# Layer 3 of a fused four-layer kernel: one key tile per work item, or two

## The chip, the cores and the metric

The kernel runs on one core of one Trainium2 chip, in one launch. Times are device microseconds of that core, from the median of three runs; the profile is of one further execution. The engines are named as the profile names them: PE (TensorE matmul) and PEld (its weight loads), ACT (ScalarE), DVE (VectorE), POOL (GpSimd) and SP (SyncE).

## The reference

Four layers follow each other on an input x of 4 images, 64 by 64 points and 64 channels, all in float32:

- layer 0: self-attention over the 4096 points of an image, with projections q, k, v; `x = gamma * out + x`
- layer 1: layer norm, pointwise and 3x3 depthwise convolutions, gates, a second layer norm and pointwise block, both with residuals
- layer 2: attention with x as query, key and value at once, in the (channel, row, column) reading of the same array; `out + x`
- layer 3: attention with 32 inner channels, then a projection back and a batch norm over all images, with a residual:

```python
f = softmax(theta_x @ phi_x.T)            # per image, 4096 x 4096
y = f @ g_x                               # 4096 x 32
w_y = y @ w_W + w_b
x + gamma * (w_y - mean) * rsqrt(var + EPS) + beta
```

The change concerns layer 3 alone.

## The kernel before, in words

The order of the work on PE, ACT and DVE is written out by hand. Each layer appends items to the list `items`; item i is called at step i, and the function `at(i, fn)` puts work into `due[i]`, which is called after item i in the same step, in the order in which it was put there. The instructions that these calls issue go into each engine's queue in that order. Two side lanes, `conv` and `misc`, hold generators (layer 1's convolutions; projections and closings of the attention layers) that are stepped between items: each item has a cost, the lanes' clocks advance by it twice per step, and a lane's next piece is issued when its clock has reached that piece's due time. `misc_from[i]` starts generators at step i; `misc_to[i]` drains the lane before it. Only the layers' order is fixed: layer 0 of all images, then layer 2 of image 0, and from there layer 2 of image b followed by layer 3 of image b − 1, and at the end layer 3 of image 3.

Layer 3 of an image runs over two halves `nb`. In each half the 2048 queries lie in four groups of 512, one for each of four row blocks of 32 partitions, and 32 key tiles `mc` of 128 keys follow each other: 64 tiles n per image. For a tile:

- `scores(n)` takes two PSUM buffers `ps` of 128x1024 from a pool of three, fills them with four matmuls of 32 rows by 128 columns (line 1314; the profile counts two instructions for each matmul), and turns each into exponentials with one ACT instruction (line 1319), both into one tile `e` of 128x2048, from a pool of six.
- `products(n)` multiplies e with g_x by four matmuls of 128 rows by 32 columns into the accumulator `y` (line 1327). The denominators of the softmax are the sums of e over all keys. For most tiles DVE adds e to a running tile, `esum` (lines 1340 and 1342); for the tiles mc = 9, 19 and 29, PE adds it instead, by four matmuls with ones into a second accumulator (line 1335).
- `totals`, once per half, adds the running tile to that accumulator with ones (line 1350), copies it out on ACT (1354), and forms the quotients on DVE (1355, 1356).
- `close` projects the result (1366), adds the bias on ACT (1368), and takes statistics on DVE (1370, 1372).

Tile n's scores are item n of the layer, cost 1.0; its products are due two items later, so PE's order is scores(n), products(n − 2), scores(n + 1), products(n − 1). Totals are due four items after the last tile of a half (two, at the end of images 0 and 1), and close eight items after it. The last tiles' products, totals and close of an image fall into the first items of what comes next. While layer 3 of image 2 runs, the lane `misc` works through `close2` and `open3` of image 3 (layer 2's normalization, and the projections that the next layer 3 needs); they are added 56 items before that layer 3 begins. `open3`'s pieces each take one more ps buffer, which DVE reads out.

Of the kernel before, what the change touches and what calls it, by code (L numbers as in the profile page):

```python
# [691 lines left out]
def fast_path(ctx: ExitStack, tc: tile.TileContext, a: dict, out: bass.AP, bad):  # L692
    nc = tc.nc
    B, H, W, C = a["x"].shape
# [16 lines left out]
    def new_ps(name="ps"):  # L711
        return pp.tile([128, 1024], F32, tag="ps", name=name)

    def new_acc(name="acc"):
        return pa.tile([128, 512], F32, tag="acc", name=name)

    def new_e(name="e"):
        return ep.tile([128, 2048], F32, tag="e", name=name)

    def new_t(name="t"):  # L720
        return tp.tile([128, 1024], F32, tag="t", name=name)

    def new_big(name):
        return big.tile([128, 4096], F32, tag="big", name=name)

    def new_pad(name="pad"):
        return big.tile([128, 66 * PW + 2], F32, tag="pad", name=name, bufs=1)
# [80 lines left out]
    for nm in names64 + names32:  # L808
        n = flat[nm].shape[0]
# [8 lines left out]
    def V(nm, i=0, lo=0, hi=128):  # L818
        k = col[nm] + i
        return vec[lo:hi, k : k + 1]  # L820
# [104 lines left out]
    def tok(x, s, j):  # L925
        return x[64 * s : 64 * s + 64, bass.ts(j, 512)]
# [4 lines left out]
    items, due = [], {}  # L931

    def at(i, fn):
        due.setdefault(i, []).append(fn)
# [316 lines left out]
    def close2(b):  # L1251
        x, m = X[:, b], im[b]
        nc.vector.tensor_reduce(sums2[:, b, :], m.zs, AX.X, ALU.add)
        rz = sm.tile([128, 32], F32, tag="rz2", name="rz2")
        nc.vector.reciprocal(rz, sums2[:, b, :])
        for i in range(4):
            d = m.ph[:, bass.ts(i, 512)].rearrange("p (w h) -> p w h", h=H)
            nc.vector.tensor_mul(d, d, rz[:, bass.ts(i, 8)].unsqueeze(2).to_broadcast([128, 8, H]))
            xs = x[:, bass.ts(i, 512)]
            nc.vector.tensor_add(xs, xs, m.ph[:, bass.ts(i, 512)])  # L1260
            yield 2.0
# [5 lines left out]
    def open3(b):  # L1267
        x, m = X[:, b], im[b]
        m.tg = new_big("tg")
        m.th = m.tg[:, 0:1024]  # L1270
        m.gx = m.tg[:, 1024:2048].rearrange("p (t d) -> p t d", d=32)
        ps = new_ps()
        for nb in range(2):
            for jj in range(2):
                mm(
                    ps[:, bass.ts(nb, 512)], thw[jj], x[:, bass.ts(2 * nb + jj, 512)],
                    start=jj == 0, stop=jj == 1,
                )
        nc.vector.tensor_scalar_add(m.th, ps, V("L3_conv_theta_b"))
        yield 3.5  # L1280
        for j in range(4):
            ps = new_ps()
            for s in range(2):
                mm(
                    ps[:, bass.ts(s, 512)], phw[64 * s : 64 * s + 64, :], tok(x, s, j),
                    start=True, stop=True,
                )
            nc.vector.tensor_scalar_add(
                m.ph[:, 0:N].rearrange("p (s n) -> p s n", s=2)[:, :, bass.ts(j, 512)],
                ps.rearrange("p (s n) -> p s n", s=2), V("L3_conv_phi_b"),  # L1290
            )
            yield 3.5
        ps = new_ps()
        for t in range(16):
            mm(ps[:, bass.ts(t, 64)], x[:, bass.ts(t, 128)], gw, start=True, stop=True)
        for s in range(2):
            nc.vector.tensor_add(
                m.gx[:, bass.ts(s, 16), :],
                ps.rearrange("p (t s d) -> p t s d", s=2, d=32)[:, :, s, :],
                gb.unsqueeze(1).to_broadcast([128, 16, 32]),  # L1300
            )
        yield 3.5

    def layer3(b):
        m, first = im[b], len(items)
        es, st = {}, {}

        def scores(n):
            nb, mc = n // 32, n % 32
            e = es[n] = new_e()  # L1310
            tiles = [new_ps(), new_ps()]
            for k in range(4):
                rows_ = slice(32 * k, 32 * k + 32)
                mm(  # L1314
                    tiles[k // 2][:, bass.ts(k % 2, 512)], m.ph[rows_, bass.ts(mc, 128)],
                    m.th[rows_, bass.ts(nb, 512)], start=True, stop=True,
                )
            for kp in range(2):
                act(e[:, bass.ts(kp, 1024)], tiles[kp], AF.Exp)  # L1319

        def products(n):
            nb, mc = n // 32, n % 32
            e, esum = es[n], m.tg[:, 2048:4096]
            if mc == 0:
                st["y"] = new_acc()
            for k in range(4):
                mm(  # L1327
                    st["y"][32 * k : 32 * k + 32, :], m.gx[:, mc, :], e[:, bass.ts(k, 512)],
                    start=mc == 0, stop=mc == 31,
                )  # L1330
            if mc % 10 == 9:
                if mc == 9:
                    st["z"] = new_acc("accz")
                for k in range(4):
                    mm(  # L1335
                        st["z"][32 * k : 32 * k + 32, :], ones[:, 0:32], e[:, bass.ts(k, 512)],
                        start=mc == 9, stop=False,
                    )
            elif mc == 1:
                nc.vector.tensor_add(esum, es[n - 1], e)  # L1340
            elif mc:
                nc.vector.tensor_add(esum, esum, e)  # L1342
            if mc == 31:
                st["yz"] = new_t("yz")
                nc.scalar.copy(st["yz"][:, 0:512], st["y"])  # L1345

        def totals():
            z, yz = st["z"], st["yz"]
            for k in range(4):
                mm(  # L1350
                    z[32 * k : 32 * k + 32, :], ones[:, 0:32], m.tg[:, 2048 + 512 * k : 2560 + 512 * k],
                    start=False, stop=True,
                )
            nc.scalar.copy(yz[:, 512:1024], z)
            nc.vector.reciprocal(yz[:, 512:1024], yz[:, 512:1024])  # L1355
            nc.vector.tensor_mul(yz[:, 0:512], yz[:, 0:512], yz[:, 512:1024])

        def close(nb):
            yz = st["yz"]
            if b % 2 == 0 and nb == 0:  # L1360
                wys["pair"] = new_big("wy") if b else new_pad("wy")
            if nb == 0:
                wys[b] = wys["pair"][:, bass.ts(b % 2, 2048)]
            ps = new_ps()
            for jj in range(2):
                mm(ps[:, bass.ts(jj, 512)], wo[jj], yz[:, 0:512], start=True, stop=True)  # L1366
            wy = wys[b][:, bass.ts(nb, 1024)]
            act(wy, ps, AF.Identity, bias=V("L3_conv_w_b"))
            for i in range(2):
                nc.vector.bn_stats(bst[:, b, nb, i, :], wy[:, bass.ts(i, 512)])  # L1370
            for i, op in enumerate((ALU.max, ALU.min)):
                nc.vector.tensor_reduce(ext3[:, b, nb, i : i + 1], yz[:, 512:1024], AX.X, op)

        for n in range(64):
            items.append((lambda n=n: scores(n), 1.0))
            at(first + n + 2, lambda n=n: products(n))
            if n % 32 == 31:
                at(first + n + (2 if n == 63 and b < 2 else 4), totals)
                at(first + n + 8, lambda n=n: close(n // 32))


    conv_from, misc_from, misc_to = {}, {}, {}
# [9 lines left out]
    for b in range(B):  # L1392
        misc_to[len(items)] = True
        f = len(items)
        layer2(b)
        more = [features2(b + 1)] if b + 1 < B else []
        if b == 0:
            misc_from[f + 16] = more
        else:
            misc_from[f + 3] = [close2(b - 1), open3(b - 1)]  # L1400
            misc_from[f + 22] = more
            misc_to[len(items)] = True
            layer3(b - 1)
    f = len(items)
    misc_from[f - 56] = [close2(B - 1), open3(B - 1)]
    misc_to[f] = True
    layer3(B - 1)

    def run():
# [83 lines left out]
    for i, (v, lo, hi) in enumerate(vals):  # L1493
        n = v.shape[1]
# [11 lines left out]
@with_exitstack  # L1506
def conv_seq_kernel(ctx: ExitStack, tc: tile.TileContext, a: dict, out: bass.AP):
    nc = tc.nc
    flag = ctx.enter_context(tc.tile_pool(name="flag", bufs=1))
    bad = flag.tile([1, 1], mybir.dt.int32, name="bad")  # L1510
    fast_path(tc, a, out, bad)
    n_bad = nc.values_load(bad[0:1, 0:1], min_val=0, max_val=1 << 20)
    with tc.If(n_bad > 0):
        general_path(tc, a, out)
# [37 lines left out]
```

## Time and profile before

| | |
|---|---|
| median of three runs | 2829.94 us (2826.72 to 2830.79) |
| the profiled execution | 2832.79 us |
| its span, first to last instruction | 2830.9 us |
| mean granted TensorE clock | 0.99 |
| busy: PE, ACT, DVE | 2746.0, 1742.7, 1443.4 us |
| layer 3 of image 0, from its first scores to the next layer's | 1675.32 to 1826.82 us |
| of image 1 | 2069.54 to 2222.47 us |
| of image 2 | 2459.45 to 2629.46 us |
| of image 3, to its last sums | 2629.46 to 2777.55 us |

A group line of the page names the source line, the engine and operation, what it writes and reads, its shape and count; then the busy time of the group and the mean of one in nanoseconds; then the engine's idle time ahead of it and what ended most of that. A timeline line has the start and the length of a merged row of instructions in microseconds, and in brackets the engine's idle time ahead of it with its releaser. Matmuls overlap, so a merged row reaches a little into the next. A line of waits has who waited, for whom, the total in microseconds, how often, and the longest.

### The profile page before, as it was taken

To read this page: it belongs to the slowest core of one execution; us is meant where nothing else is said; L and a number is where in the kernel's file an instruction comes from. 1 tells how busy PE (TensorE), PEld (TensorE's weight loads), DVE (VectorE), ACT (ScalarE), POOL (GpSimd) and SP (SyncE) were. 2 spreads that over 40 slices of the span, in tenths; PEclk is the share of its full clock that TensorE was granted. 3 is DMA by queue.
4 is the path that set the end of the run, shared out by engine and by line. 5 is a ranking of instruction groups with operands and counts; after the bars stand their busy time and mean duration, and the time that the engine had idled before them with its cause. 6 is when DMAs were issued, how large, how long until landed. Compare 5 with 4: busy or idle time off the path is not lost.

```text
span 2830.9 us, 41626 instructions
## 1 busy us (share of the span) xinstructions
PE 2746.0 (97%) x17950; PEld 929.1 (33%) x17950; DVE 1443.4 (51%) x1551; ACT 1742.7 (62%) x2807; POOL 21.5 (1%) x77
## 2 busy tenths in 40 slices
PE   8999999999999999989999999999999999999995
PEld 3343333333333333322333332243322333322222
DVE  3232488435794348521772128920068610198896
ACT  4545555555655565556645568845678656678884
POOL 2000000000000000000000000000000000000000
PEclk9999999999999999999999999999999999999997
DMA  4000000000000000000000000000000000000002
GB/s 70 1 1 1 1 1 1 1 0 1 1 1 1 1 0 1 1 1 1 1 1 1 1 1 1 1 1 1 1 1 1 1 1 1 1 1 1 1 1 61
DMA packets 18500, 11.80 MB, mean 4 GB/s; under 512 B 1436, under 2 KB 18181, under 8 KB 18309
## 3 DMA queue, kind: packets, MB, share of 16 engines
q1 hardware_dynamic: 16085, 7.89, 1.3%
q8 instruction: 142, 2.33, 0.3%
q10 hardware_dynamic: 1296, 0.56, 0.1%
q0 software_dynamic: 928, 0.62, 0.1%
q14 instruction: 49, 0.40, 0.0%
HBM read 4.87 MB, written 4.19 MB: 3 GB/s over the span
## 4 chain that ended last, share of the span: by engine, by line
PE 90%; DVE 6%; ACT 3%; issue 1%; DMA 0%; ACTq 0%; DVEq 0%; POOL 0%; POOLq 0%
PE acc L1034 16%; PE ps L1010 16%; PE acc L1224 16%; PE ps L1207 15%; PE ps L1314 9%; PE acc L1327 7%; DVE tg L1342 2%; PE ps L1161 2%; PE ps L1104 1%; PE ps L1061 1%; DVE yz L1355 1%; ACT e L1319 1%; PE ps L1366 1%; PE accz L1335 1%; PE ps L987 1%
## 5 line engine op out<-in xcount | busy, mean ns | idle before, releaser
L1014 ACT ACTIVATE e<-ps 128x1024 f32<-128x1024 f32 x512 | 516.9, 1024 | 343.2 <-PE ps L1010 208.9
L1215 ACT ACTIVATE e<-ps 128x1024 f32<-128x1024 f32 x512 | 517.0, 1024 | 317.3 <-PE ps L1207 316.9
L1319 ACT ACTIVATE e<-ps 128x1024 f32<-128x1024 f32 x512 | 495.9, 1023 | 110.4 <-PE ps L1314 92.0
L1342 DVE TENSOR_TENSOR tg<-tg,e 128x2048 f32<-128x2048 f32 x216 | 494.9, 2291 | 26.2 <-ACT e L1319 8.2
L1010 PE MATMUL ps<-X,q 64*128 64x512 f32 x2048 | 491.2, 606 | 13.4 <-ACT e L1014 4.2
L1207 PE MATMUL ps<-ko 64*64 64x512 f32 x4096 | 474.6, 596 | 18.1 <-ACT ko L1190 8.7
L1224 PE MATMUL acc<-e,X 64*64 64x512 f32 x4096 | 469.0, 593 | 0.6 <-ACT yz L1345 0.6
L1034 PE MATMUL acc<-e,vq 128*64 128x512 f32 x2048 | 468.4, 599 | 0.0
L1314 PE MATMUL ps<-tg,ph 32*128 32x512 f32 x2048 | 320.7, 640 | 5.6 <-ACT e L1319 4.2
L1041 DVE SCALAR_TENSOR_TENSOR yv<-acc,gam,yv 128x512 f32<-128x512 f32 x224 | 167.4, 749 | 242.8 <-PE acc L1034 231.3
L1010 PEld LDWEIGHTS ps<-X,q 64*128 64x128 f32 x2048 | 190.4, 186 | 293.6 <-issue 185.5
L1327 PE MATMUL acc<-e,tg 128*32 128x512 f32 x2048 | 272.4, 604 | 1.3 <-ACT yz L1345 1.3
L1207 PEld LDWEIGHTS ps<-ko 64*64 64x64 f32 x4096 | 152.5, 133 | 314.1 <-issue 196.8
L1224 PEld LDWEIGHTS acc<-e,X 64*64 64x64 f32 x4096 | 157.3, 133 | 282.6 <-issue 272.5
L1034 PEld LDWEIGHTS acc<-e,vq 128*64 128x64 f32 x2048 | 136.5, 137 | 312.0 <-issue 290.2
L1232 DVE TENSOR_TENSOR ph<-ph,acc 128x512 f32<-128x512 f32 x16 | 11.0, 687 | 389.1 <-ACT ph L1231 389.1
L1314 PEld LDWEIGHTS ps<-tg,ph 32*128 32x128 f32 x2048 | 102.5, 183 | 223.5 <-issue 147.3
L1126 DVE SCALAR_TENSOR_TENSOR y<-pad,vec,y 128x1024 f32<-128x1024 f32 x128 | 164.3, 1283 | 7.6 <-ACT pad L1109 3.5
L1126 DVE SCALAR_TENSOR_TENSOR yg<-pad,vec,yg 128x1024 f32<-128x1024 f32 x128 | 164.3, 1283 | 3.8
L1014 ACT ACTIVATION_READ_ACCUMULATOR e<-ps 128x1 f32 x512 | 106.0, 207 | 0.0
L1215 ACT ACTIVATION_READ_ACCUMULATOR e<-ps 128x1 f32 x512 | 106.0, 207 | 0.0
L1327 PEld LDWEIGHTS acc<-e,tg 128*32 128x32 f32 x2048 | 41.0, 108 | 196.3 <-issue 190.6
(177 smaller groups left out, 1221.9 us busy)
## 6 DMA issues: line engine op xcount, KB each, us to landing
out_dram<-o SPq DMA_DIRECT2D x16, 256.0 KB
xr<-in_x_dram SPq DMA_DIRECT2D x14, 256.0 KB
xr<-in_x_dram ACTq DMA_DIRECT2D x2, 256.0 KB
pw<-in_L_conv_pw_w_dram POOLq DMA_DIRECT2D x4, 64.0 KB, 4.9
phw<-in_L_conv_phi_W_dram POOLq DMA_DIRECT2D x8, 8.0 KB, 1.8
sca<-in_L_conv_sca_w_dram POOLq DMA_DIRECT2D x1, 64.0 KB, 6.3
pw<-in_L_conv_pw_w_dram POOLq DMA_DIRECT2D x2, 32.0 KB, 5.3
thw<-in_L_conv_theta_W_dram POOLq DMA_DIRECT2D x4, 8.0 KB, 2.1
```

What stands on the lines that cost most here:

```text
L1010: mm(ps[:, bass.ts(r, 512)], m.q[rows_, bass.ts(t, 128)], x[rows_, bass.ts(g, 512)], start=True, stop=True,)
L1014: act(es[g // 2][:, bass.ts(g % 2, 1024)], ps, AF.Exp, bias=SHIFT0, accum_out=zs[:, g : g + 1],)
L1034: mm(accs[g][64 * r : 64 * r + 64, :], vq, es[half][:, 1024 * g + 512 * r : 1024 * g + 512 * r + 512], start=t == 2 * p, stop=t == 2 * p + 1,)
L1041: stt((x if p == 15 else m.y)[:, cols], accs[g], gam0, (m.y if p else x)[:, cols], ALU.mult, ALU.add,)
L1126: stt(out_, win, wt, out_, ALU.mult, ALU.add)
L1207: mm(ps[64 * c : 64 * c + 64, bass.ts(r, 512)], m.ko[rows_, 128 * jb + 64 * c : 128 * jb + 64 * c + 64], m.ko[rows_, bass.ts(2 * ib + r, 5 ...
L1215: act(es[n, jb], ps, AF.Exp, bias=SHIFT2, accum_out=m.zs[:, jb, ib : ib + 1])
L1224: mm(acc[r][64 * c : 64 * c + 64, :], xw[rows_, jb, :], es[n, jb][rows_, bass.ts(c, 512)], start=jb == 0, stop=jb == 31,)
L1314: mm(tiles[k // 2][:, bass.ts(k % 2, 512)], m.ph[rows_, bass.ts(mc, 128)], m.th[rows_, bass.ts(nb, 512)], start=True, stop=True,)
L1319: act(e[:, bass.ts(kp, 1024)], tiles[kp], AF.Exp)
L1327: mm(st["y"][32 * k : 32 * k + 32, :], m.gx[:, mc, :], e[:, bass.ts(k, 512)], start=mc == 0, stop=mc == 31,)
L1342: nc.vector.tensor_add(esum, esum, e)
```

## The change

An item of layer 3 now holds two key tiles: their scores are issued one after the other, and in the same step the products of the two tiles in front. The tiles that PE sums are mc = 4, 9, 14, 19, 24 and 29, six per half in place of three, so DVE adds three tiles fewer. An item costs 2.0 on the lanes' clocks, so a tile costs what it did. Distances in items are halved: products come one item later, totals two (one, at the end of images 0 and 1), close four, and the lane work for image 3 is added 28 items ahead. Pools, tiles and shapes of all instructions stay.

```diff
-            if mc % 10 == 9:
-                if mc == 9:
+            if mc % 5 == 4:
+                if mc == 4:
                     st["z"] = new_acc("accz")
                 for k in range(4):
                     mm(
                         st["z"][32 * k : 32 * k + 32, :], ones[:, 0:32], e[:, bass.ts(k, 512)],
-                        start=mc == 9, stop=False,
+                        start=mc == 4, stop=False,
                     )
...
-        for n in range(64):
-            items.append((lambda n=n: scores(n), 1.0))
-            at(first + n + 2, lambda n=n: products(n))
-            if n % 32 == 31:
-                at(first + n + (2 if n == 63 and b < 2 else 4), totals)
-                at(first + n + 8, lambda n=n: close(n // 32))
+        for n in range(0, 64, 2):
+            i = first + n // 2
+            items.append((lambda n=n: [scores(n), scores(n + 1)], 2.0))
+            at(i + 1, lambda n=n: [products(n), products(n + 1)])
+            if n % 32 == 30:
+                at(i + (1 if n == 62 and b < 2 else 2), totals)
+                at(i + 4, lambda n=n: close(n // 32))
...
-    misc_from[f - 56] = [close2(B - 1), open3(B - 1)]
+    misc_from[f - 28] = [close2(B - 1), open3(B - 1)]
```

## The prediction, made before the changed kernel had run

> **What bounds the kernel now.** I read the page first, then the windows of layer 3's stages, then the PE and ACT timelines inside one stage, then single instruction starts. The page:
>
> ```profile
> PE 2746.0 (97%) x17950; PEld 929.1 (33%) x17950; DVE 1443.4 (51%) x1551; ACT 1742.7 (62%) x2807; POOL 21.5 (1%) x77
> PE 90%; DVE 6%; ACT 3%; issue 1%; DMA 0%; ACTq 0%; DVEq 0%; POOL 0%; POOLq 0%
> L1319 ACT ACTIVATE e<-ps 128x1024 f32<-128x1024 f32 x512 | 495.9, 1023 | 110.4 <-PE ps L1314 92.0
> L1342 DVE TENSOR_TENSOR tg<-tg,e 128x2048 f32<-128x2048 f32 x216 | 494.9, 2291 | 26.2 <-ACT e L1319 8.2
> ```
>
> PE carries 90% of the chain. In layer 3 the other engines are close behind: one key tile needs two exps (1.02 us each) and, mostly, one DVE add of 2.29 us. The PE and ACT timelines in the middle of a stage:
>
> ```profile
> 1740.90 1.21 PE L1314 MATMUL ps<-tg,ph 32*128 32x512 f32 x8
> 1742.04 1.07 PE L1327 MATMUL acc<-e,tg 128*32 128x512 f32 x8
> 1743.03 1.25 PE L1314 MATMUL ps<-tg,ph 32*128 32x512 f32 x8
> 1744.21 1.07 PE L1327 MATMUL acc<-e,tg 128*32 128x512 f32 x8
> 1745.20 1.21 PE L1314 MATMUL ps<-tg,ph 32*128 32x512 f32 x8
> ```
>
> ```profile
> 1739.90 1.94 ACT L1319 ACTIVATE e<-ps 128x1024 f32<-128x1024 f32 x2 [0.19 <-PE ps L1314]
> 1742.07 1.94 ACT L1319 ACTIVATE e<-ps 128x1024 f32<-128x1024 f32 x2 [0.24 <-PE ps L1314]
> ```
>
> A tile costs 2.155 us (four tiles from 1738.72 to 1747.34), and scores and products alternate: about 1.14 to 1.18 from start to start, then 0.99. Two things matter. Scores starting at 1740.90 reach ACT at 1742.07, so an exp begins 1.17 us after its scores begin (1.23 elsewhere). And the scores are already touched by buffers: each tile fills two of the three ps buffers, so a tile's second buffer is the one that the previous tile's first exp must leave. In the trace that exp ends at 1740.924 and the matmul into its buffer starts at 1740.978, 0.08 us behind its partner. The products in between hide the rest. The waits of layer 3's first stage name it:
>
> ```profile
> PEld ps L1314 <- ACT e L1319: 17.1, 21, 1.6
> ```
>
> Where an exp is later (behind DVE's reciprocal at a close), the hole is open:
>
> ```profile
> 1766.37 1.13 PE L1314 MATMUL ps<-tg,ph 32*128 32x512 f32 x4
> 1768.23 1.13 PE L1314 MATMUL ps<-tg,ph 32*128 32x512 f32 x4 [0.73 <-ACT e L1319]
> 1769.29 1.98 PE L1366 MATMUL ps<-yz,wo 128*128 128x512 f32 x4
> ```
>
> The tile's first half ran, its second half waited for an exp, and PE did nothing else meanwhile. A half alone occupies 1769.29 − 1768.23 = 1.06 us, as much as a whole tile (1.07), because the four matmul groups of a tile otherwise run side by side.
>
> [...] products follow each other every 0.43 us within their kind, 0.54 before a switch. [...]
>
> **The change, part by part.**
>
> *Scores of two tiles back to back.* They need four ps buffers, A, B, C, D; the pool has three, so D is A's buffer. From the start of A and B, at 0: exp A starts at 1.20 (mean of 1.17 and 1.23), lasts 1.02, and 0.05 later D may start, at 2.27. C starts at 0.97 on one half of the rows and cannot take D's place. D needs 1.06: scores end at 3.33. Without the wait D would start beside C at 0.97; so it loses 1.30. Queued behind D in PE's order are the previous pair's products; ACT, with exps B and C in hand (C's ends near 4.0), then D's to 5.0, waits for the next pair.
>
> *Products of two tiles back to back.* 0.88 + 0.98 = 1.86 (0.88 is the length of products followed by the same mode, as before the sums L1335). Pair: 3.33 + 1.86 = 5.19 against 2 × 2.155 = 4.31. The next pair's buffers are all free by then (exps B, C, D end at 3.1, 4.0, 5.0), so this repeats. 4 images × 32 pairs × 0.88 = **+112.6**.
>
> *Three more sums on TensorE per half image.* 4 × 2 × 3 = 24 more blocks of L1335, each 0.88 + 0.97 − 0.99 = 0.86: **+20.6**. They take away 24 DVE adds of 2.29 (55 us of DVE), worth nothing here: DVE then has at most 4.7 us of adds in a pair of 5.19. Were DVE the bound, they would give back 3 × 2.29 = 6.9 us per half image.
>
> *What before loses and after does not.* Five closes inside layer 3 stall the scores (2.92 in place of about 1.17): −8.8. Two of those lower the clock for a window, L1366 x4 then taking 3.61 in place of 1.91: −3.4. At the end L1350 waits 5.34 for the backlog of adds and then runs 1.94 in place of 0.88; a pair's DVE work now fits its period: −6.4. One block of products at 2513.73 takes 2.45 in place of 1.00: −1.4. The first tiles of three stages wait 0.4 and 0.9: −3.9. Sum **−23.9**.
>
> *Moved steps.* Totals come after the next pair's scores, then DVE's reciprocal and multiply (3.35 + 0.69) go ahead of two pairs' adds. From the scores before the totals: the copy of z ends at 5.6, the reciprocal block at 9.7, the adds free their e tiles at 12.1 and 14.4. With six e tiles the exps three pairs on want them at 12.4 and 14.3: 0.1 late, and no matmul sees it. If the reciprocal block came late once more, 2 us a time over five closes, +10: the upper end. The turn of layer 2's last block waits for a copy now behind four exps in ACT's order instead of two; the pair's scores of 3.3 us cover it. The image-3 projections are added 28 items ahead rather than 56, which is the same 56 tiles; each now holds a fifth buffer, evacuated by DVE (1.28) between adds: 4.7 + 1.3 = 6.0 in a pair that a projection's matmuls (1.06 at least) make 6.25 long, so zero, with +8 the upper end. No DMA is issued in these stages; SP's and POOL's queues stay as they were. At the end of the first two images, totals stand one item earlier, behind the following layer's 3.6 us of scores: −0.4 each, left out.
>
> 112.6 + 20.6 − 23.9 = **+109**. The profiled execution took 2832.79 (span 2830.9 and 1.9 around it) and becomes 2942; the median of the runs shown is 2.85 below it, so 2829.94 + 109 = **2939**.
>
> **Bounds.** No view of before shows D's wait in a steady stage. Lower: its weights may load while it waits (second pass after 0.43 in place of 0.53), −13; exp start at 1.17, −4. Upper: exp start at 1.23, +4; +10; +8. I take the values above because the hole at 1766 shows a waiting half with its whole 1.06. Ends: 2922 and 2961.
>
> **Rivals.**
> - *D's wait is hidden, fewer switches win (4%).* One mechanism: D finding its buffer empty at 0.97. Then scores take 1.93, products 1.86, and four exps (3.77 at 1767.15) bind at about 3.9: 128 × (3.9 − 4.31) + 20.6 − 23.9 = −56, so 2774. It decides where D waits less than 1.30 − 109/128 = 0.45 us. Against it: three buffers, and an exp of 1.02 that cannot begin before 1.17.
> - *Half of the wait (5%).* If the first half's exp could start as soon as its own matmuls were done, well before 1.17, and D with it, about 55 us would remain: 2885. Against it: at 2076.52 a lone first half still waited 1.23 for its exp.
> - *DVE and e tiles late as well (7%).* Closes and projections stall as today, or worse: +130 to +170, 2960 to 3000. For it: today's five stalls come from exactly there; against it: 24 adds fewer and a longer period.
> - *The clock falls (4%).* [...] The windows view, where columns end with granted clock, DMA share and GB/s:
>
> ```profile
> 2160.14:2163.55 3.41, 2.68 (x17) 0.63 (x9) 3.38 (x2) 2.17 (x3) 0.00 (x0) 1.00 0.01 2
> 2163.55:2166.97 3.42, 3.42 (x6) 1.12 (x4) 3.28 (x3) 1.60 (x2) 0.00 (x0) 0.50 0.00 0
> ```
>
>   Two of the five holes did this. Layer 3's stages take 622 us today and would take some 730, 214 windows of 3.41 us; if it befell one in three, 71 × 1.7 = +121 more, 3060. Against it: a hole there leaves PE empty for about 0.9 us; in a pair C fills all but 0.4, and three of the five holes of before cost no clock.
>
> That the change does not do what it says is out: in the changed program's order each pair's eight score matmuls stand together, the fourth buffer's first one with a wait on ACT.
>
> **How the numbers follow.** The forecast case has 80%, its own range being the bounds. The range 2920 to 2962 adds only rounding; outside lie the fast rival, the half wait, the clock and most of the DVE case, about 2 in 10. Within 0.2% (5.7 us, about what a measurement of this kernel can tell from no change) needs a chance cancellation: 1%. Faster 4%, slower 95%.
>
> **What would show it.** In the changed profile: scores in two blocks per pair, the second half of the second tile about 2.3 us after the first start, PE waiting for ACT e there in nearly every pair; starts of pairs 5.2 apart, 6.05 with a sum; ACT idle 1.3 us per pair on PE; L1342 x192; L1335 x384; no wait of L1350 for DVE. Pairs at 4.0 with ACT never idle would prove me wrong; so would a granted clock below 0.97, or exps waiting for DVE.

## The result and the profile after

The changed kernel took 2935.8 us (median of four runs, 2932.3 to 2940.7) against 2830.4 for the kernel before (2826.7 to 2832.9): a ratio of 1.0375, with a 95% interval of 1.0355 to 1.0394. It is slower, by 105 us.

The same lines of the page as were shown of before, in the kernel after:

```profile
PE 2822.9 (96%) x18142; PEld 963.5 (33%) x18142; DVE 1388.9 (47%) x1527; ACT 1730.9 (59%) x2807; POOL 21.5 (1%) x77
PE 89%; ACT 6%; DVE 3%; issue 1%; DMA 0%; ACTq 0%; POOL 0%; DVEq 0%; POOLq 0%
L1319 ACT ACTIVATE e<-ps 128x1024 f32<-128x1024 f32 x512 | 482.8, 1030 | 234.1 <-PE ps L1314 218.3
L1342 DVE TENSOR_TENSOR tg<-tg,e 128x2048 f32<-128x2048 f32 x192 | 439.9, 2291 | 138.5 <-ACT e L1319 128.6
```

PE's busy time rose by 77 us and its share hardly moved, 97% to 96%. By that line alone one would call PE a little more loaded. The other two engines say more: ACT's idle time ahead of the exps of layer 3 went from 110 to 234 us, and DVE's ahead of its adds from 26 to 138. ACT now waits for PE's scores and DVE for ACT's exps, and in the chain ACT's share has doubled, from 3% to 6%. The timeline says why. PE and then ACT, in the middle of a stage of image 0 in the kernel after:

```profile
1735.94 1.99 PE L1314 MATMUL ps<-tg,ph 32*128 32x512 f32 x12
1738.19 1.13 PE L1314 MATMUL ps<-tg,ph 32*128 32x512 f32 x4 [0.27 <-ACT e L1319]
1739.25 1.92 PE L1327 MATMUL acc<-e,tg 128*32 128x512 f32 x16
1741.10 1.99 PE L1314 MATMUL ps<-tg,ph 32*128 32x512 f32 x12
1743.35 1.13 PE L1314 MATMUL ps<-tg,ph 32*128 32x512 f32 x4 [0.27 <-ACT e L1319]
1744.41 1.06 PE L1327 MATMUL acc<-e,tg 128*32 128x512 f32 x8
1745.29 1.04 PE L1335 MATMUL accz<-e,ones 128*32 128x512 f32 x8
1746.15 1.04 PE L1327 MATMUL acc<-e,tg 128*32 128x512 f32 x8
1747.12 1.99 PE L1314 MATMUL ps<-tg,ph 32*128 32x512 f32 x12
```

```profile
1737.11 3.77 ACT L1319 ACTIVATE e<-ps 128x1024 f32<-128x1024 f32 x4 [1.39 <-PE ps L1314]
1742.28 3.77 ACT L1319 ACTIVATE e<-ps 128x1024 f32<-128x1024 f32 x4 [1.39 <-PE ps L1314]
```

A pair is 1741.10 − 1735.94 = 5.16 us, and 6.02 with a sum (1747.12 − 1741.10), where two tiles took 4.31 before. The scores of a pair are one row of twelve instructions (buffers A, B and C) and one of four (D). D starts 2.25 after the pair, just behind the end of the pair's first exp (start 1737.11, 1.02 long), and the products stand behind D. Over the whole run the score matmuls stood idle for the exps, and their weight loads for longer:

```profile
PE ps L1314 <- ACT e L1319: 36.1, 124, 0.6
PEld ps L1314 <- ACT e L1319: 198.6, 197, 1.4
```

In the kernel before, the matmuls' idle time for the exps was 4.2 us, and the row of the weight loads reads 72.1 us in 85 waits. Neither sum is the 105 us that the run lost; what a wait costs is read from the length of a pair.

Stretch by stage, the two profiled executions (2832.79 and 2932.31, so +99.5) differ like this. Layer 3, from its first scores to its last totals, took 2784.80 − 1675.32 = 1109.5 and takes 2885.52 − 1667.60 = 1217.9 (layer 2 of two images lies in both): +108.4. The tail behind it went from 46.1 to 45.0: −1.1. All ahead of layer 3 is the same program and was 7.7 us shorter in the execution after; two stretches of lowered clock near 965 and 1610 us in the execution of before (10.2 and 6.8 us long, granted 0.50) are missing there. That part is a difference between executions and not of the change.

At the end of the kernel, where L1350 had waited for DVE's backlog of adds, nothing waits any more. PE's timeline of the kernel before, and then of the kernel after:

```profile
2784.80 1.94 PE L1350 MATMUL accz<-tg,ones 128*32 128x512 f32 x8 [5.34 <-DVE tg L1342]
```

```profile
2883.54 1.90 PE L1327 MATMUL acc<-e,tg 128*32 128x512 f32 x16
2885.52 1.06 PE L1350 MATMUL accz<-tg,ones 128*32 128x512 f32 x8
```

### The profile page after: what moved, and what is told of

It reads as the page before. It is cut to its first block, busy times and chain, and to the rows that moved or that the text cites. A ratio compares the mean times of both kernels' runs of the same rounds, so it can differ in the third digit from the quotient of the medians.

```text
span 2930.5 us, 41966 instructions
## 1 busy us (share of the span) xinstructions
PE 2822.9 (96%) x18142; PEld 963.5 (33%) x18142; DVE 1388.9 (47%) x1527; ACT 1730.9 (59%) x2807; POOL 21.5 (1%) x77
## 4 chain that ended last, share of the span: by engine, by line
PE 89%; ACT 6%; DVE 3%; issue 1%; DMA 0%; ACTq 0%; POOL 0%; DVEq 0%; POOLq 0%
PE acc L1034 15%; PE ps L1010 15%; PE acc L1224 15%; PE ps L1207 15%; PE ps L1314 9%; PE acc L1327 8%; ACT e L1319 4%; PE ps L1161 2%; PE accz L1335 1%; PE ps L1104 1%; PE ps L1061 1%; PE ps L1366 1%; PE ps L1284 1%; PE ps L987 1%; PE var L1070 1%
## 5 line engine op out<-in xcount | busy, mean ns | idle before, releaser
L1342 DVE TENSOR_TENSOR tg<-tg,e 128x2048 f32<-128x2048 f32 x192 | 439.9, 2291 | 138.5 <-ACT e L1319 128.6
L1314 PE MATMUL ps<-tg,ph 32*128 32x512 f32 x2048 | 398.2, 627 | 37.4 <-ACT e L1319 36.1
L1327 PE MATMUL acc<-e,tg 128*32 128x512 f32 x2048 | 250.5, 598 | 0.0
L1314 PEld LDWEIGHTS ps<-tg,ph 32*128 32x128 f32 x2048 | 127.0, 183 | 309.5 <-ACT e L1319 198.6
L1327 PEld LDWEIGHTS acc<-e,tg 128*32 128x32 f32 x2048 | 54.0, 109 | 170.4 <-issue 170.3
```

Source lines behind the costliest of these rows:

```text
L1314: mm(tiles[k // 2][:, bass.ts(k % 2, 512)], m.ph[rows_, bass.ts(mc, 128)], m.th[rows_, bass.ts(nb, 512)], start=True, stop=True,)
L1327: mm(st["y"][32 * k : 32 * k + 32, :], m.gx[:, mc, :], e[:, bass.ts(k, 512)], start=mc == 0, stop=mc == 31,)
```

## The experiments

The theory is the prediction's: the pair's fourth ps buffer comes free only with the pair's first exp, and the products behind it wait too. The rivals are that the sums or the items' coarser steps cost the time (the closes, the lanes, DVE's turn), that the idle time at D is the whole loss, or that the clock suffers.

### The two halves of the change apart

The change with the three sums of before:

```diff
-            if mc % 5 == 4:
-                if mc == 4:
+            if mc % 10 == 9:
+                if mc == 9:
...
```

> The pairs alone: items of two tiles as in the change, but PE sums only tiles 9, 19 and 29 of 32 as before. Theory (the fourth ps buffer waits for the pair's first exp): 24 blocks of sums at 0.86 us fall away from 2936, so about 2915, with pairs still starting every 5.16 us. Rival (the sums are what costs): near 2830. Rival (DVE is nearly the bound, and the sums pay for themselves): 2936 or more, with exps waiting for DVE.

Measured: 2912.87 (2911.12 to 2917.05), 1.0298 of before (1.0281 to 1.0315). The pairs are 5.16 apart as in the full change. So the pairs carry some 82 of the 105 us, and three more sums per half add 23 (0.86 × 24 = 20.6 by the timeline).

The kernel before with the six sums of the change:

```diff
-            if mc % 10 == 9:
-                if mc == 9:
+            if mc % 5 == 4:
+                if mc == 4:
...
```

> The sums alone: items of one tile as before, PE sums six tiles of 32. Theory: +20.6 us for 24 blocks, of which up to 20 come back because DVE is no longer late at the closes and at the end: 2830 to 2850, with the five stalls of the scores at the closes shorter or gone. Rival (the sums are what costs): near 2936.

Measured: 2836.74 (2835.66 to 2839.84), 1.0029 (1.0018 to 1.0040), which is 7.6 us slower than before. Of the 20.6 that the sums cost, DVE's shorter backlog gives back about 13: the last products with the wait behind them go from 7.24 to 2.84, and each of the five closes stalls 0.86 less but is not cured; these make 8.7. The two windows of lowered clock at the closes are gone as well (L1366 x4 takes 1.91 at all five), which is 3.4, and L1350 at the end runs 0.88 shorter. PE's timeline at the first close:

```profile
1765.44 2.13 PE L1314 MATMUL ps<-tg,ph 32*128 32x512 f32 x8
1767.50 1.98 PE L1366 MATMUL ps<-yz,wo 128*128 128x512 f32 x4
```

These scores, 2.92 to the next work in the kernel before, are still 2.06 here.

### The order alone

All of the change but its order: items of two tiles, six sums, halved distances, with scores and products alternating within an item as before.

```diff
-            items.append((lambda n=n: [scores(n), scores(n + 1)], 2.0))
-            at(i + 1, lambda n=n: [products(n), products(n + 1)])
+            items.append((lambda n=n: [scores(n), n and products(n - 2), scores(n + 1), n and products(n - 1)], 2.0))
...
```

The first item of an image has no products in front, so its two tiles stay back to back; the last two tiles' products follow one item later, as in the change.

> Items of two tiles, six sums and halved distances as in the change, but inside an item the order of before: scores, products, scores, products. Theory: no fourth ps buffer is needed at once, the wait goes, and the time is that of the sums alone, 2830 to 2842. Rival (items of two with their halved distances and lane steps cost something by themselves): 2850 to 2936.

Measured: 2827.83 (2823.48 to 2832.64), 0.9999 (0.9989 to 1.0009), a little under what was expected. In this form the second half's first add overwrites the running tile before the first half's totals have read it, so it changes the denominators. A second form puts the totals of the first half (n = 34) between that item's scores and products:

```diff
+            def item(n=n):
+                scores(n)
+                if n == 34:
+                    totals()
+                n and products(n - 2)
+                scores(n + 1)
+                n and products(n - 1)
...
+            items.append((item, 2.0))
...
```

> Items of two tiles, six sums and halved distances as in the change, but inside an item the order of before: scores, products, scores, products; the first half's totals stand between, ahead of the next half's products, so that the running sum is read before it is begun anew. Theory: two ps buffers at a time are enough, the wait goes, and the time is that of the sums alone (2836.7), a few us less where totals come a tile earlier: 2828 to 2840. Rival (items of two, halved distances and lane steps cost something by themselves): 2850 to 2936.

Measured: 2828.49 (2824.36 to 2832.68), 0.9999 (0.9990 to 1.0007). PE's timeline of this kernel:

```profile
1736.47 1.14 PE L1314 MATMUL ps<-tg,ph 32*128 32x512 f32 x8
1737.54 1.06 PE L1327 MATMUL acc<-e,tg 128*32 128x512 f32 x8
1738.54 1.31 PE L1314 MATMUL ps<-tg,ph 32*128 32x512 f32 x8
1739.78 1.06 PE L1327 MATMUL acc<-e,tg 128*32 128x512 f32 x8
1740.78 1.15 PE L1314 MATMUL ps<-tg,ph 32*128 32x512 f32 x8
```

Two tiles take 1740.78 − 1736.47 = 4.31 again, and the five closes no longer stall: here L1366 stands behind the item's products, and the scores ahead of them take 1.07. The six sums and the vanished stalls cancel to −1.1 us, which is less than the noise. The order of the eight score matmuls within a pair is worth the rest, 2935.8 − 2828.5 = 107 us. It differs in 124 of the 128 pairs (all but the first of each image), so that is 0.87 a pair. The rival of the coarser steps falls: items of two, later closes and the lane work added 28 items ahead cost nothing that can be measured.

### Is it the exp that D waits for?

Three kernels change what stands between A's scores and D. The first lets ACT take the pair's second exp ahead of its first:

```diff
-            for kp in range(2):
+            for kp in (0, 1) if n % 2 else (1, 0):
                 act(e[:, bass.ts(kp, 1024)], tiles[kp], AF.Exp)
```

> The changed kernel, but ACT takes the exp of the pair's second ps buffer ahead of that of the first; nothing else is altered. Theory: the fourth buffer's matmuls wait one exp longer (0.92 us from start to start), ACT itself has 1.3 us to spare in a pair, so 128 x 0.92 = +118 on 2936: about 3054, pairs every 6.08 us. Rival (the pair's length is set by PE's mode switches or by anything but this exp): 2936.

Measured: 2942.59 (2938.99 to 2943.24), 1.0394 (1.0377 to 1.0411). I was wrong: the wait did not become two exps long. PE and ACT in this kernel:

```profile
1731.25 1.99 PE L1314 MATMUL ps<-tg,ph 32*128 32x512 f32 x12
1733.59 1.13 PE L1314 MATMUL ps<-tg,ph 32*128 32x512 f32 x4 [0.36 <-ACT e L1319]
```

```profile
1732.52 3.77 ACT L1319 ACTIVATE e<-ps 128x1024 f32<-128x1024 f32 x4 [1.48 <-PE ps L1314]
```

B's exp runs first, ends at 1733.54, and D starts 0.05 later, 0.86 before A's exp ends. So D cannot be in A's buffer: it had been given the one that is released first, B's this time. So the edit didn't test what it was meant to. It shows only that D follows the end of the pair's first exp, whichever buffer that one reads.

The second doubles the suspected wait: the first exp is done twice.

```diff
-            for kp in range(2):
+            for kp in (0, 1) if n % 2 else (0, 0, 1):
```

> The changed kernel with the exp of each pair's first ps buffer done twice in a row (the same values are written again). Whichever buffer is released first is then released one exp later, 0.92 us from start to start, and ACT, with five exps in a pair, still has over a microsecond to spare. Theory: the fourth buffer's matmuls start 3.2 us after the pair in place of 2.3, pairs every 6.08 us, 128 x 0.92 = +118: about 3054. Rival (ACT's time is not in the pair's loop): within 10 us of 2936.

Measured: 3120.0 (3111.9 to 3126.9), 1.1041 (1.1017 to 1.1066), further than expected. PE's timeline:

```profile
1742.54 1.99 PE L1314 MATMUL ps<-tg,ph 32*128 32x512 f32 x12
1745.85 1.13 PE L1314 MATMUL ps<-tg,ph 32*128 32x512 f32 x4 [1.32 <-ACT e L1319]
```

D moved from 2.25 to 3.31 after the pair's start, 1.06 later, which is one more exp (the second began 1.055 after the first). 128 pairs × 1.055 = 135 us follow from the wait. The rest is the clock. Two pairs of neighbouring windows of this kernel (the first time after the length is PE's busy time; columns end with granted clock, DMA share and GB/s):

```profile
1708.04:1711.45 3.41, 2.09 (x18) 0.75 (x14) 0.33 (x1) 2.15 (x3) 0.00 (x0) 1.00 0.00 0
1711.45:1714.86 3.41, 3.41 (x28) 0.93 (x28) 2.46 (x2) 2.65 (x3) 0.00 (x0) 1.00 0.00 0
1721.69:1725.10 3.41, 2.09 (x14) 0.69 (x10) 2.29 (x1) 2.50 (x3) 0.00 (x0) 1.00 0.00 0
1725.10:1728.51 3.41, 3.41 (x16) 0.60 (x16) 1.00 (x1) 2.38 (x3) 0.00 (x0) 0.50 0.00 0
```

After the second window with 2.09 us of busy time PE ran at half the clock, after the first it did not, so busy time alone does not decide it; what does was not shown. Layer 3 of this kernel has 26 windows at half the clock, each by my estimate 1.7 us dearer (half of its 3.41), 44 us in all. For the two profiled executions the sum is 2932.3 + 135 + 44 = 3111, and 3111.9 was measured.

The third takes the cause away: the first exp of each pair is left out. This kernel leaves out a quarter of layer 3's exps, and products, sums and adds take the tile's other half twice in their place, so that all other instructions stay.

```diff
-            for kp in range(2):
+            for kp in range(0 if n % 2 else 1, 2):
...
-                    st["y"][32 * k : 32 * k + 32, :], m.gx[:, mc, :], e[:, bass.ts(k, 512)],
+                    st["y"][32 * k : 32 * k + 32, :], m.gx[:, mc, :], e[:, bass.ts(k if n % 2 else 2 + k % 2, 512)],
...
```

> The changed kernel without the exp of each pair's first ps buffer (a quarter of layer 3's exps is left out, and products and sums take the tile's other half twice). Nothing reads that buffer, so the fourth one is free at once. Theory: scores of a pair take 1.93 in place of 3.31, pairs start every 3.79 us, 128 x (3.79 - 5.16) = -175: about 2760, up to 15 more where DVE's adds (4.7 us in a pair without a sum) now bind. Rival (the half-filled third and fourth buffers or the switches set the pair): 2900 or more.

Measured: 2804.42 (2802.92 to 2808.62), 0.9908 (0.9892 to 0.9925). The loss is gone, though the kernel is 44 us slower than I expected. PE's timeline:

```profile
1717.31 2.32 PE L1314 MATMUL ps<-tg,ph 32*128 32x512 f32 x16
1719.56 1.92 PE L1327 MATMUL acc<-e,tg 128*32 128x512 f32 x16
1721.42 2.32 PE L1314 MATMUL ps<-tg,ph 32*128 32x512 f32 x16
```

A pair's scores are one row of 2.25 and the pair 4.11, so 128 × (4.11 − 5.16) = −134 us: 2801. The scores aren't 1.93 because D starts at 1.195 (2.25 less the 1.06 that it takes alone) and not at 0.97. What holds it back that far, with the first exp gone, was not shown.

### Is it the idle time at D?

The trace of the changed kernel shows PE idle for only some 0.3 us at D, a third of what a pair loses. A kernel that fills the wait with work puts the first tile's products between C and D:

```diff
+                scores(n)
+                first = half_scores(n + 1)
...
+                n and products(n - 2)
+                half_scores(n + 1, first)
+                n and products(n - 1)
...
```

> The changed kernel with one tile's products moved into the wait: PE does three ps buffers of scores, products, the fourth buffer, products. Nothing waits then, but the third and fourth buffers still run alone, about as long as a whole tile each, and there are four switches again: 1.93 + 0.99 + 1.06 + 0.99 = 4.97 per pair in place of 5.16, so 2936 - 24 = about 2912. Rival (the wait alone is the loss): filling it brings back all of it, 2840 or less.

Measured: 2915.34 (2914.15 to 2915.71), 1.0302 (1.0286 to 1.0318). PE's timeline, in which L1314 is the first tile's scores, L1328 each half of the second's, and L1341 the products:

```profile
1736.69 1.14 PE L1314 MATMUL ps<-tg,ph 32*128 32x512 f32 x8
1737.65 1.02 PE L1328 MATMUL ps<-tg,ph 32*128 32x512 f32 x4
1738.61 1.07 PE L1341 MATMUL acc<-e,tg 128*32 128x512 f32 x8
1739.60 1.13 PE L1328 MATMUL ps<-tg,ph 32*128 32x512 f32 x4
1740.66 1.06 PE L1341 MATMUL acc<-e,tg 128*32 128x512 f32 x8
1741.66 0.71 PE L1314 MATMUL ps<-tg,ph 32*128 32x512 f32 x4
```

No hole is left, and the pair still takes 4.97. The two halves C and D, 0.96 and 1.06 from start to next start, each cost what the whole first tile costs (0.96). Filling the hole brought 0.19 a pair, although this order has four changes between scores and products in a pair, where the changed kernel has two. The order of before has four as well, and takes 4.31. The difference of 0.66 is what it costs to part C from D, with no idle time at all.

### A version that beats both

The stalls at the closes of before had shown up in the prediction's ledger, and half of the change's sums didn't cure them. Two kernels on the order of before ask what does. First, four sums at mc = 3, 6, 17 and 29:

```diff
-            if mc % 10 == 9:
-                if mc == 9:
+            if mc in (3, 6, 17, 29):
+                if mc == 3:
...
```

> The kernel before with four sums of 32 on PE, tiles 3, 6, 17 and 29. Eight blocks of 0.86 us cost 6.9; two of the sums stand just behind DVE's reciprocal block, so the five stalls of the scores at the closes (8.8, and 3.4 of lowered clock) and most of the wait at the end (6.4) should go: 2815 to 2826. If the stalls come from the reciprocal block alone and not from the backlog of adds: 2836.

Measured: 2827.63 (2824.71 to 2830.54), 0.9996 (0.9988 to 1.0005): no difference, and above what was expected. The close's scores still take 2.06; the shorter backlog pays for the eight added sums and no more.

Then the three sums of before, with the totals two items after a half's last tile everywhere, as the ends of images 0 and 1 have it already:

```diff
-                at(first + n + (2 if n == 63 and b < 2 else 4), totals)
+                at(first + n + 2, totals)
```

> The kernel before with every half's totals due two items after its last tile in place of four. DVE's order is the same, but its reciprocal no longer idles 7.7 us for the copy of the sums: it starts about 4.3 us sooner, e tiles come free sooner, and the five stalls at the closes go: 12 us less, 2815 to 2820. If PE now waits for DVE's last add at the totals: 2825 to 2835.

Measured: 2819.55 (2816.42 to 2821.80), 0.9968 (0.9956 to 0.9980): 10 us faster than before, and faster than the changed kernel by 116. DVE's and ACT's timeline at the first close in the kernel before, then DVE's and PE's in this one:

```profile
1760.76 3.35 DVE L1355 RECIPROCAL yz<-yz 128x512 f32<-128x512 f32 x1 [7.72 <-ACT yz L1354]
1767.15 3.77 ACT L1319 ACTIVATE e<-ps 128x1024 f32<-128x1024 f32 x4 [1.97 <-DVE tg L1340]
```

```profile
1756.50 3.35 DVE L1355 RECIPROCAL yz<-yz 128x512 f32<-128x512 f32 x1 [3.51 <-ACT yz L1354]
```

```profile
1766.23 1.30 PE L1314 MATMUL ps<-tg,ph 32*128 32x512 f32 x8
1767.46 1.98 PE L1366 MATMUL ps<-yz,wo 128*128 128x512 f32 x4
```

DVE had stood idle for 7.72 us waiting for the totals' copy. Now it idles for 3.51, the reciprocal starts 4.26 earlier, and the adds behind it free their e tiles in time for the exps. In the kernel before, exps waited for DVE's add at each of the five closes, 9.9 us in all; in this kernel none does. The close's scores take 1.23 in place of 2.92, in all five closes.

Last, the same with the sums at mc = 10, 21 and 31, so that the last tile of a half needs no add:

```diff
+            if mc in (10, 21, 31):
+                if mc == 10:
...
+                at(first + n + 2, totals)
```

> The kernel before with totals due two items after the last tile, and the three sums on PE at tiles 10, 21 and 31 in place of 9, 19 and 29: the last tile of a half then needs no DVE add, so the wait for DVE at the very end (3.9 us with early totals) shrinks by up to 2.3 and the totals of the other halves stand less. 2814 to 2819.6; if the longer stretch of 10 adds before the last sum makes DVE late inside the half, 2820 to 2825.

Measured: 2818.91 (2816.23 to 2822.97), 0.9965 (0.9952 to 0.9979). The two kernels can't be told apart by their times, and the wait that was to shrink did not: at the end L1350 waits 3.67 us for DVE in place of 3.87, and from the start of the last scores to the totals it is 8.76 in place of 8.70.

A fourth ps buffer, with which D would not need to wait for an exp, was not tried.

## Why the prediction was right

**The fourth buffer's wait: right.** The prediction put D at 2.27, the end of the scores at 3.33, the products at 1.86 and the pair at 5.19. The trace has 2.25, 3.31 (3.37 where the exp starts at 1.23 in place of 1.17), 1.85 and 5.16. The step was +112.6 for 128 pairs, or 109 for the 124 in which the order alone differs; that measures 107. Without the first exp the median fell by 131 us; with a second one the profiled execution grew by 180 us, of which the clock took some 44. Both times that is about 128 times what the timeline shows of D.

**The sums: right.** 0.86 each, as the step has it: 6.02 − 5.16. The 55 us of DVE adds that they remove bought no time of their own. Where the order is unchanged they gave back 13 of their 20.6 us through the backlog at the closes and the end.

**The stalls that vanish: right within the noise.** The step said −23.9. Six sums at the old order in items of two came out at −1.1 against before, with an interval of some 2.5 us either way, although the first pair of each image still waits for the fourth buffer in that kernel, about 4.5 us in all. So the stalls were worth 20.6 + 4.5 + 1.1, about 26, give or take 2.5. In the trace after, the scores ahead of L1366 take 3.36, an ordinary pair's; L1350 runs 2 us after the last products start; and between its first scores and last totals no window of layer 3's stages has a lowered clock (granted 1.00).

**The moved steps: right at zero.** No close, no projection of image 3 (L1275 3.63, L1284 1.06 each, L1295 3.71) and no turn to the next layer makes a pair longer than its own work. Behind four of the projections the buffer C waits for DVE's copy (0.31 us of idle time), but the pair's scores still take 3.31, since D, which waits for the exp, ends last. The copies and exps that come later had the pair's 3.3 us of scores to hide behind.

**Layer 3 as a whole.** +109 by the sum, +108.4 in the trace. Against the median the forecast of 2939 is 3 us high, which is less than the spread of the runs.

**What was off: what the wait costs, if it were gone.** The prediction said "Without the wait D would start beside C at 0.97; so it loses 1.30", and built the fast rival's 2774 on it. With the exp taken away D started at 1.195, and the pair gained 1.05. The sum didn't rest on that sentence, since it was made from where D starts and how long it runs alone. Neither is the loss the idle time that a wait suggests: filling the hole recovered 20 us of the 107 (in medians, 2935.8 − 2915.3), and that order has two more changes between scores and products in a pair (a tile's products take 0.99 ahead of scores and 0.88 ahead of sums). What the split loses is that C and D no longer run side by side. In the kernel before, the four row groups of the tile at 1740.90 start within 0.085 us of each other; parted, D starts 1.29 after C in the changed kernel. A half tile alone takes 1.06, a whole one 0.96 to 1.07.

**The rivals.** *DVE late*: the trace shows DVE waiting for ACT, 128.6 us where it was 8.2, so it was the more idle engine. *Half of the wait*: the exp starts 1.17 after the scores, as before. *The clock*: the granted clock was 0.994. But a lower clock was near: with 1.32 us of hole a pair in place of 0.27 the granted clock was 0.978, and 26 windows of 3.41 us at half the clock took some 44 us, by the estimate above.

## What to carry to other kernels

Before putting two units of work back to back, count the buffers that both hold at once. Here one was missing: D stood until the first exp's end, 2.25 us after its pair's start, and the products behind it until 3.31. The price could be read from the start of that exp, its length and the length of what then runs alone, all in the old trace. Where small matmuls run side by side, look at how they are split before looking at idle time: here a half alone took 1.06 us, a whole tile 0.96 to 1.07. And where an engine waits several microseconds for an input that could be issued earlier, as DVE did for the totals (7.72 us), look at that first: moving that issue by two items gained 10 us here, and moving adds from DVE to PE gained nothing.

## What the runs showed of the hardware

- Two of a tile's four row groups alone took 1.06 us, all four 0.96 to 1.07. Parting them by other work cost 0.66 us a pair with no idle time (4.97 where it was 4.31).
- A repeated exp into the same output began 1.055 us after the first, where exps into different outputs follow each other at 0.92 (four in 3.77, five with the repeated one in 4.83). What held it was not shown.
- With the pair's first exp left out, D started 1.195 us after its pair, where the prediction had 0.97. What held it was not shown.
- With holes of 0.29 us on average in the pairs (36.1 us in 124 waits, the longest 0.6), the granted clock was 1.00 throughout layer 3. With holes of 1.32 us, 26 windows of 3.41 us were at half the clock. Of two windows in which PE was busy for 2.09 us, the one at 1721.69 was followed by such a window and the one at 1708.04 was not. What decides it was not shown.
